# Two cross-attention layers in fp32: the keys' bias sums folded by VectorE and summed by one short product, and the last rows copied in two parts

## The chip, the cores and the metric

The kernel runs on one core of a Trainium2 chip. The metric is the device time of one execution in microseconds (us). Before the change three executions took 582.25, 584.28 and 584.83 us; the median, 584.28, stands for the kernel.

The engines are named as the profile names them: PE (TensorE, matrix products; PEld are its weight loads), DVE (VectorE), ACT (ScalarE), POOL (GpSimd) and SP (SyncE, which here only issues transfers). SBUF is the on-chip memory, 128 partitions wide; PSUM is what PE writes to, in banks of 128 by 512 fp32 numbers.

## The reference

Two layers of cross-attention run one after the other. A batch has 100 tokens of width E = 1024 and 1444 context rows of width L = 512; there are 8 batches. All is fp32.

```
layer 0:  Q = x Wq + bq,  K = ctx Wk + bk,  V = ctx Wv + bv
          x = x + softmax(Q K' / 32, over keys) V Wo + bo
layer 1:  q, k, v in the same way, from the new x, with layer 1's weights
          w = softmax(q k' / 32, over axis 1)          (over the TOKENS, for each key)
          x = layernorm(w v + x) * gamma + beta
```

Layer 1 takes its softmax over the tokens. So what depends on the token alone doesn't cancel in it: the term of the keys' bias, x·(Wq bk) + bq·bk, is needed for each of the 800 tokens. In layer 0 the same term shifts a whole softmax; the kernel still carries it into the shift of the exponent.

## The kernel before, in words

**Products are rearranged.** Scores are (x (Wq Wk') + u) ctx', so the keys are never projected: `weight_products` makes Wq Wk' for each layer ("qk0", "qk1") and Wv Wo for layer 0 ("vo0"), and `queries` multiplies it by x (g0T and g1T in the profile, 512 features by 2 groups of 400 tokens). Large products use seven block products in place of eight (Strassen in Winograd's form): `left_sums`, `right_sums` and `inner_product` have DVE form the sums of blocks, PE the seven products X, Z, Y, W and so on, and DVE and ACT add the results to their places (`add`, `put`).

**Stages in PE's order**, which is the order of the program (`manual_schedule`): qk0, vo0, queries of layer 0, qk1 (137 to 184 us); scores and weighted sums of layer 0 (185 to 319); its output product and the queries of layer 1 (310 to 388, and g_y later); scores and weighted sums of layer 1 with output products between them (388 to 573).

**A batch of attention.** `scores_by_keys` computes the 1444 by 100 scores in 12 blocks of 128 keys (the last has 36), four contraction steps each, into three PSUM banks; blocks stand in two halves of the array at once, so a batch is 184 matmul records (s, L965). It is a generator that stops after each block, except after the very last, after which it goes on to set up the softmax. `weighted_rows` multiplies the weights by the context rows (A, 192 records, L915). `alternated` takes one step of A of batch b and one of s of batch b + 2 in turn.

**The keys' bias.** `key_bias_sums` has DVE (in layer 0 ACT as well, with a transfer that adds the two parts) form kb[p, t] = sum over c of xT[p, c, t] wqbk[p, c], with 128 partitions by 800 tokens. What is wanted is the sum over the 128 partitions, in every partition. `key_bias_rows` (L651 to L657) does that with two products of an all-ones 128 by 128 matrix by 400 columns, and DVE scales each and adds bq·bk while it copies it back to kb (in the profile: PE `kb<-kb,ones` L656, and DVE `kb<-kb,bqbk`; all DVE instructions that go through the object `vector` have line L100, so they are told apart by their tiles).

In layer 0 this happens behind qk1 (L853, L854), ahead of the first scores. In layer 1 it happens inside the scores of batch 0: after 46 of the 48 steps come the two products, then the last two steps (L1472 to L1475), then what remains of the queries (g_y, L1476), then the scores of batch 1.

**Sums in every partition by 32 by 32 blocks.** For other sums the kernel has a second way: `block_sums` (L592) transposes in 32 by 32 blocks and reduces, and `totals` (L603) multiplies the result by `same`, a 0/1 matrix with same[p, j] = 1 where p and j agree modulo 32 (L606). DVE's transpose works on each 32 by 32 block by itself.

**Orders.** PE runs in the program's order. The order of the other engines is a planner's, from its own costs, except where `vector.in_order` is true or `keep_in_program_order` is called: those instructions keep the program's order among themselves. Transfers of the context are all issued on SP's queue in program order (`loaded_in_order`, L862); transfers that add into a tile are POOL's (`transfer_added`, L579). PSUM has two pools: `bank` (6 banks, in which scores and most products live) and `bank2` (2 banks). A bank is taken at the first use of its tile and is free after the last.

**qk1's `between`.** `weight_products` calls `between` (L539, L540) while the inner product W runs, after DVE has formed the operands of the inner product Q (`last`). For qk1 it did nothing. DVE is in the program's order there.

**The end.** `weighted_rows` of the last batch copies its 400 columns (4 chunks of 100 tokens) from PSUM with one ACT copy (L927); `project_last` then multiplies the last 128 rows by wv in three column parts (ol, L1371: 383 + 1, 512 and 129 columns, four contraction steps each, one for a chunk), and DVE, ACT and POOL normalise and store them.

Of the kernel before, what the change touches and what calls it, by code (L numbers as in the profile page):

```python
# [25 lines left out]
F32 = mybir.dt.float32  # L26
AF = mybir.ActivationFunctionType
ALU = mybir.AluOpType
AX = mybir.AxisListType
PE = mybir.EngineType.PE  # L30

P = 128
HP = P // 2
B, T, E = 8, 100, 1024
S, L = 1444, 512
EC, LC = E // P, L // P
NQ = 4
MC = 12
CQ = MC // NQ
GM = 4  # L40
QD = 32
G = 4
GT = G * T
# [5 lines left out]
KEYS = (8, 11, 9, 10, *range(8))  # L49
LAST = (MC - 1) * P  # L50
PAD = S - LAST + QD
SCALE = 1.0 / math.sqrt(E)
# [4 lines left out]
def two_layer_cross_attention(ctx: ExitStack, tc: tile.TileContext, a: dict, out: bass.AP):  # L57
    nc = tc.nc
# [5 lines left out]
    small = ctx.enter_context(tc.tile_pool(name="small", bufs=2))  # L64
# [4 lines left out]
    def bank(name):  # L69
        return psum.tile([P, 512], F32, tag="ps", name=name)  # L70
# [34 lines left out]
    vector = Vector()  # L105


    ones = const.tile([P, P], F32, tag="ones", name="ones")
# [7 lines left out]
    same = const.tile([P, P], F32, tag="same", name="same")  # L116
# [28 lines left out]
    def run(*parts):  # L145

        parts = list(parts)
        while parts:
            parts = [g for g in parts if next(g, parts) is not parts]
# [442 lines left out]
    def block_sums(name, t, sums, late=False):  # L592

        ins = nc.vector.transpose(t, t)
        if late:
            tc.keep_in_program_order(ins)  # L600
        nc.vector.tensor_reduce(sums, t.rearrange("p (c q i) -> p c q i", q=P // QD, i=QD), AX.X, ALU.add)

    def totals(name, sums, n):  # L603

        ps = bank(name)[:, : n * P // QD]
        nc.tensor.matmul(ps, same, sums.rearrange("p c q -> p (c q)"), start=True, stop=True)  # L606
        own = small.tile([P, 2 * EC, P // QD], F32, tag="own", name=f"{name}_own", bufs=1)[:, :n, :]
        mask = quarter.unsqueeze(1).to_broadcast([P, n, P // QD])
        nc.vector.tensor_tensor(own, ps.rearrange("p (c q) -> p c q", q=P // QD), mask, ALU.mult)
        got = const.tile([P, n], F32, tag=name, name=name)  # L610
        nc.vector.tensor_reduce(got, own, AX.X, ALU.add)
        return got

    def quarter_sums(name):
        return small.tile([P, 2 * EC, P // QD], F32, tag="sums", name=f"{name}_sums")

    def bias_products():

        part = small.tile([P, 2], F32, tag="bbs", name="bbs")
        for layer in range(2):  # L620
            prod = small.tile([P, EC], F32, tag="bb", name=f"bb{layer}")
            nc.vector.tensor_tensor(prod, cols[f"L{layer}_xattn_bq"], cols[f"L{layer}_xattn_bk"], ALU.mult)
            nc.vector.tensor_reduce(part[:, layer : layer + 1], prod, AX.X, ALU.add)
        ps = bank("bb_ps")
        nc.tensor.matmul(ps[:, :2], ones, part, start=True, stop=True)
        got = const.tile([P, 2], F32, tag="bqbk", name="bqbk")
        nc.vector.tensor_scalar(got, ps[:, :2], SCALE, None, ALU.mult)
        return got[:, 0:1], got[:, 1:2]

    def key_bias_sums(name, wqbk, tiles=()):  # L630

        acc = to = work.tile([P, B * T], F32, tag="kb", name=name, bufs=1)

        def steps():
            if tiles:
                scaled_sum(tiles, [(xT[:, k, :], wqbk[:, k : k + 1]) for k in range(EC)])
            for k in range(len(tiles), EC):  # L640
                if k == len(tiles):
                    vector.tensor_scalar(to, xT[:, k, :], wqbk[:, k : k + 1], None, ALU.mult)
                else:
                    vector.scalar_tensor_tensor(to, xT[:, k, :], wqbk[:, k : k + 1], to, ALU.mult, ALU.add)
                yield
            if tiles:
                transfer_added(to, tiles[0])

        return acc, steps()

    def key_bias_rows(kb, bqbk):  # L651

        for g in range(B // G):
            rows = kb[:, g * GT : (g + 1) * GT]
            ps = bank(f"kb_{g}")[:, :GT]
            nc.tensor.matmul(ps, ones, rows, start=True, stop=True)  # L656
            vector.tensor_scalar(rows, ps, SCALE, bqbk, ALU.mult, ALU.add)  # L657

    def queries(layer, w, u, between=None):

# [156 lines left out]
    bqbk0, bqbk1 = bias_products()  # L817
# [11 lines left out]
    for g in range(B // G):  # L829
# [9 lines left out]
    gT[0], steps = queries(  # L839
        0, wqk0, totals("u0", sums_u, LC), lambda: block_sums("bvo", acc_o, sums_c[:, EC:, :], late=True)  # L840
    )
    qk1 = weight_products(
        "qk1", "L1_xattn_WqT", "L1_xattn_WkT", E, L, (("L1_xattn_bk", 0), ("L1_xattn_bq", 1)), lambda: None
    )
    run(islice(steps, 2))
    next(qk1)
# [4 lines left out]
    kb0, more = key_bias_sums("kb0", wqbk0[:, :EC], [t[:, : B * T] for t in prob])  # L851
    run(more)
    wqk1, (acc_c, acc_u) = next(qk1)  # L853
    key_bias_rows(kb0, bqbk0)  # L854
    sums = quarter_sums("k1")

    def add_out_bias(e):
# [49 lines left out]
    def weighted_rows(s, layer, c, dst):  # L907

        b, w = s["b"], s["w"]
        ps = bank2(f"A{layer}_{b}")  # L910
        for m in range(MC):
            r = max(keys(m), PAD)
            for k in range(LC):
                for h in both_sides():
                    nc.tensor.matmul(  # L915
                        ps[h * HP : (h + 1) * HP, k * T : (k + 1) * T],
                        c[m // CQ][:r, m % CQ, k * P + h * HP : k * P + (h + 1) * HP],
                        w[:r, m, :],
                        start=(m == 0 and k == 0),
                        stop=(m == MC - 1),  # L920
                        skip_group_check=True,
                    )
                if (m, k) == (MC - 1, LC - 1):
                    src = ps[:, :GT].rearrange("p (c t) -> p c t", t=T)
                    if layer:
                        for to, part in dst:
                            ins = nc.scalar.copy(to, src[:, :, part])  # L927
                            if s["b"] == B - 1:
                                tc.keep_in_program_order(ins)
                    else:  # L930
                        divided(s, ps, dst, src)
                yield
# [13 lines left out]
        nc.vector.reciprocal(r, ps[:, GT : GT + T])  # L946
        nc.vector.tensor_tensor(dst, src, r.unsqueeze(1).to_broadcast([P, LC, T]), ALU.mult)

    def scores_by_keys(s, layer, cT, softmax):

        b = s["b"]
        q = gT[layer][b // G]
        t0 = b % G * T
        banks = [bank(f"s{layer}_{b}_{n}") for n in range(MC // GM)]
        rest = []
        for k in range(LC):
            for m in KEYS:
                whole = keys(m) == P
                n = HP if whole else keys(m)
                for h in both_sides() if whole else one_side():  # L960
                    o = m * P + h * HP if whole else m * P
                    to = banks[m // GM][h * HP : h * HP + n, m % GM * T : (m % GM + 1) * T]
                    if k >= LC - 2 and not whole:
                        rest.append(to)
                    nc.tensor.matmul(  # L965
                        to,
                        cT[k][:, o : o + n],
                        q[:, k, t0 : t0 + T],
                        start=(k == 0 and m % GM == 0),
                        stop=(k == LC - 1 or (k == LC - 2 and not whole)),  # L970
                        skip_group_check=True,
                    )
                if (k, m) != (LC - 1, KEYS[-1]):
                    yield
        w = weight_rows(f"w{layer}_{b}")
        s["w"] = w[:, : MC * T].rearrange("p (c t) -> p c t", t=T)
        nc.gpsimd.memset(s["w"][:PAD, MC - 1, :], 0.0)  # L977
        s["softmax"] = softmax(s, [blocks_of(banks, ms) for ms in ROWS], rest)
        for _ in islice(s["softmax"], LATER.get((layer, b))):
            pass  # L980
        yield
# [408 lines left out]
    batches = [{"b": b} for b in range(B)]  # L1390
# [22 lines left out]
    cT = [list(load_features(0)), list(load_features(1, (2,)))]  # L1413
# [39 lines left out]
    kb1, more = key_bias_sums("kb1", wqbk1)  # L1453
# [4 lines left out]
            next(more, None)  # L1458
    run(more)
    vector.in_order = False  # L1460
    wv1 = weights.tile([P, LC, E], F32, tag="w", name="wv1")
    nc.gpsimd.dma_start(out=wv1, in_=a["L1_xattn_Wv"].rearrange("(c p) e -> p c e", p=P))


    cT = [list(load_features(0, parts=4)), list(load_features(1, (2,), 4))]
    result = out.rearrange("b t e -> (b t) e")
    n = TILES[-1][0] // 6
# [1 line left out]
        loaded_in_order(result[i * n : (i + 1) * n], a["L1_xattn_beta"].partition_broadcast(n))  # L1469
    tiles = [{"t0": t0, "n": n} for t0, n in TILES]  # L1470
    turned = turned_blocks(tiles)
    scores1 = scores_by_keys(batches[0], 1, cT[0], softmax1)  # L1472
    run(islice(scores1, LC * MC - 2))
    key_bias_rows(kb1, bqbk1)
    run(scores1)  # L1475
    run(steps)  # L1476
    run(scores_by_keys(batches[1], 1, cT[1], softmax1))
# [9 lines left out]
    for b in range(B):  # L1487
        parts = []
        for last, _, tokens in SETS:
# [6 lines left out]
            to = homes[last][:, :, lo - tokens.start : hi - tokens.start]  # L1496
# [52 lines left out]
```

## Time and profile before

| | us |
|---|---|
| median of three executions | 584.28 |
| the profiled execution's own time | 581.93 |
| its span, first to last instruction | 580.2 |
| PE busy in the span | 569.4 |
| DVE busy | 429.0 |
| ACT busy | 145.3 |
| POOL busy | 122.6 |
| PE records on the bias products (L656), 8 of them, together | 3.1 |

The profile is one execution. Its times run from the span's start. A row of a timeline has the start, the length, the engine, the line, the operation, the tiles (result <- operands), the shape, and how many instructions were merged; in brackets stands how long the engine had been idle before it and what released it. A matmul's end is modelled and overlaps the next one's start, so distances between starts are what PE's work costs. An fp32 matmul stands as two records. PE's granted clock is 1.00 in every stretch from 185 to 556 us and 0.91 in the last 24 us. Single instructions can be read with a timeline of one engine in a short window; groups of the same instruction with the list of groups.

### The profile page before, as it was taken

The numbers are of one execution on the slowest core, as the hardware profiler recorded it, in microseconds if no ns is written. First come the engines' busy times: TensorE is split into PE (matmuls) and PEld (weight loads), VectorE is DVE, ScalarE is ACT, GpSimd is POOL, SyncE is SP. The second block draws the span as 40 slices with busy tenths as digits, with TensorE's granted clock in tenths as the row PEclk, the third lists the DMA queues.
The fourth block names the chain that finished last, engine by engine and source line by source line (L and its number), as shares of the span: only waits on it lengthen the run. The fifth ranks groups of instructions, "written<-read, shape, count | busy, mean of one in ns | idle before, by whom it ended". The sixth has DMA issues, their size and how long they took to land.

```text
span 580.2 us, 17218 instructions
## 1 busy us (share of the span) xinstructions
PE 569.4 (98%) x7280; PEld 473.4 (82%) x7280; DVE 429.0 (74%) x990; ACT 145.3 (25%) x379; POOL 122.6 (21%) x189
## 2 busy tenths in 40 slices
PE   9999999999999999999999999999999999999994
PEld 8887457678899999999998856677999869959672
DVE  1997579879587684784559786895568769969855
ACT  1331321432250112101211000013333036236532
POOL 3110110221120142052223000000423313404412
PEclk9999999999999999999999999999999999999998
DMA  9959989944399999999999004886899958996704
GB/s 281 313 106 320 311 205 280 311 79 97 68 234 335 348 388 372 331 371 374 366 353 304 2 0 160 263 282 203 247 298 337 361 171 292 295 285 205 204 2 92
DMA packets 74125, 142.83 MB, mean 246 GB/s; under 512 B 8384, under 2 KB 30144, under 8 KB 74048
## 3 DMA queue, kind: packets, MB, share of 16 engines
q1 hardware_dynamic: 66592, 120.62, 60.8%
q0 software_dynamic: 7024, 20.59, 17.9%
q8 instruction: 57, 0.93, 0.6%
q10 hardware_dynamic: 432, 0.52, 0.3%
q14 instruction: 20, 0.16, 0.1%
HBM read 124.28 MB, written 6.03 MB: 225 GB/s over the span
## 4 chain that ended last, share of the span: by engine, by line
PE 76%; issue 6%; DMA 5%; POOL 1%; DVE 1%; ACT 1%; POOLq 0%; DVEq 0%
PE s L965 22%; PE A L915 21%; PE g_x L168 5%; PE qk_x L168 4%; PE o_x L168 3%; PE o_x L1211 3%; DMA vo_L_xattn_bv<-vo_L_xattn_bv 2%; DMA g_t<-xT 2%; PE g_y L168 2%; PE o_y L1211 2%; PE o_y L168 1%; PE qk_z L168 1%; PE qk_y L168 1%; PE o_w L1211 1%; PE o_z L1211 1%
## 5 line engine op out<-in xcount | busy, mean ns | idle before, releaser
L915 PE MATMUL A<-w,c 128*64 128x100 f32 (+1 forms) x3072 | 226.9, 249 | 0.0
L915 PEld LDWEIGHTS A<-w,c 128*64 128x64 f32 (+1 forms) x3072 | 202.4, 137 | 1.7 <-issue 1.7
L965 PE MATMUL s<-g0T,cT 128*64 128x100 f32 (+1 forms) x1472 | 112.8, 250 | 1.1 <-issue 0.8
L965 PE MATMUL s<-g1T,cT 128*64 128x100 f32 (+1 forms) x1472 | 113.5, 250 | 0.3 <-issue 0.3
L965 PEld LDWEIGHTS s<-g0T,cT 128*64 128x64 f32 (+1 forms) x1472 | 100.9, 136 | 2.8 <-issue 2.2
L965 PEld LDWEIGHTS s<-g1T,cT 128*64 128x64 f32 (+1 forms) x1472 | 97.4, 136 | 2.3 <-issue 1.7
L1178 POOL TENSOR_TENSOR part<-w 128x500 f32<-128x500 f32 x16 | 26.9, 1682 | 155.4 <-DVE rtotal L100 88.4
L1158 ACT ACTIVATE w<-w,negmax 128x100 f32<-128x100 f32 x96 | 35.0, 366 | 56.0 <-DVE negmax L100 55.9
L1026 ACT ACTIVATE w<-w 128x400 f32<-128x400 f32 (+2 forms) x32 | 12.0, 442 | 119.6 <-DVE w L100 119.6
L100 DVE STREAM_TRANSPOSE z<-xT 32x256 f32<-32x256 f32 x88 | 38.3, 435 | 1.3
L100 DVE TENSOR_REDUCE most<-s 128x100 f32<-128x400 f32 (+1 forms) x24 | 12.5, 521 | 35.7 <-PE s L965 35.7
L168 PE MATMUL qk_x<-qk 128*128 128x256 f32 x128 | 30.4, 386 | 0.0
L168 PEld LDWEIGHTS qk_x<-qk 128*128 128x128 f32 x128 | 23.9, 195 | 3.1 <-ACT qk L442 0.2
L100 DVE SCALAR_TENSOR_TENSOR w<-s,kb 128x400 f32<-128x400 f32 (+2 forms) x32 | 13.8, 463 | 11.7 <-PE s L965 11.5
L977 POOL MEMSET w<- 68x100 f32 x16 | 3.8, 238 | 68.1 <-PE A L915 28.3
L1158 ACT ACTIVATION_READ_ACCUMULATOR w<-w,negmax 128x1 f32 x96 | 18.0, 188 | 0.0
L676 ACT ACTIVATE g1T<-g_x,k 128x400 f32<-128x400 f32 x4 | 2.4, 593 | 59.4 <-PE g_x L168 59.2
L1181 POOL TENSOR_TENSOR part<-part 128x100 f32<-128x100 f32 x32 | 16.5, 516 | 2.5
L100 DVE TENSOR_TENSOR w<-w,rtotal 128x400 f32<-128x400 f32 (+2 forms) x32 | 15.0, 469 | 1.1
L580 POOL DMA_DIRECT2D qk_L_xattn_bk<-qk_L_xattn_bk x6 | 5.2, 923 | 48.1 <-DMA qk_L_xattn_bk<-qk_L_xattn_bk 20.1
L168 PE MATMUL vo_x<-vo 128*128 128x512 f32 x32 | 15.3, 595 | 0.0
L1330 POOL TENSOR_TENSOR rstd<-rstd,mhalf 128x1 f32<-128x1 f32 (+2 forms) x6 | 8.2, 1370 | 28.2 <-DVE rstd L100 22.3
(448 smaller groups left out, 1031.9 us busy)
## 6 DMA issues: line engine op xcount, KB each, us to landing
c<-in_ctx SPq DMA_DIRECT2D x176, 256.0 KB
cT<-in_ctxT SPq DMA_DIRECT2D x96, 176.0 KB
cT<-in_ctxT SPq DMA_DIRECT2D x32, 370.0 KB
cT<-in_ctxT SPq DMA_DIRECT2D x32, 352.0 KB
cT<-in_ctxT SPq DMA_DIRECT2D x32, 194.0 KB
vo<-in_L_xattn_Wo SPq DMA_DIRECT2D x8, 512.0 KB
qk<-in_L_xattn_WqT SPq DMA_DIRECT2D x8, 512.0 KB
qk<-in_L_xattn_WqT SPq DMA_DIRECT2D x15, 256.0 KB
```

Of the source, the lines that this page charges most:

```text
L100: ins = getattr(nc.vector, op)(*args, **kw)
L168: nc.tensor.matmul(banks[n // per][:, n % per * width : (n % per + 1) * width], lhs[i][:, n * P : (n + 1) * P], rhs[i], start=(fresh and i ...
L580: nc.gpsimd.dma_start(out=to, in_=t, accum_op=ALU.add)
L915: nc.tensor.matmul(ps[h * HP : (h + 1) * HP, k * T : (k + 1) * T], c[m // CQ][:r, m % CQ, k * P + h * HP : k * P + (h + 1) * HP], w[:r, m, :],
L965: nc.tensor.matmul(to, cT[k][:, o : o + n], q[:, k, t0 : t0 + T], start=(k == 0 and m % GM == 0), stop=(k == LC - 1 or (k == LC - 2 and no ...
L977: nc.gpsimd.memset(s["w"][:PAD, MC - 1, :], 0.0)
L1026: nc.scalar.activation(rows, rows, AF.Exp)
L1158: nc.scalar.activation(rows[:, i, :], rows[:, i, :], AF.Exp, bias=negmax[:, i : i + 1], accum_out=total[:, i : i + 1])
L1178: add(part, w[:, 0:5, :], w[:, 5:10, :], ALU.add)
L1181: add(part[:, 0, :], part[:, 0, :], more, ALU.add)
L1211: nc.tensor.matmul(ps[:n, :], lhs[0][:, i, :], rhs[0][:, i, :], start=(fresh and i == 0), stop=(i == 1), skip_group_check=True,)
L1330: nc.gpsimd.tensor_tensor(rstd, rstd, mhalf[:n], ALU.pow)
```

## The change

The two 400-column products with all ones become one product of 25 columns with `same`. For that, DVE first folds kb: it transposes kb in 32 by 32 blocks in place and reduces each block's 32 columns to one, which gives `part`, 128 by 25: partition 32 r + i has, for block n, the sum over quarter r's partitions for token 32 n + i. The product with `same` adds the four quarters. DVE scales the 25 columns and spreads them back: one transpose in 32 by 32 blocks whose input repeats each of the 25 columns 32 times.

The fold is a function of its own, called earlier than the product: in layer 0 in qk1's `between`, in layer 1 after the sums of kb are complete. In layer 1 the product now comes after all 48 score steps of batch 0 (`hold` makes the generator stop after the last block as well). And the last batch's copy of rows is made in two ACT copies of two chunks each.

```diff
-    def key_bias_rows(kb, bqbk):
-
-        for g in range(B // G):
-            rows = kb[:, g * GT : (g + 1) * GT]
-            ps = bank(f"kb_{g}")[:, :GT]
-            nc.tensor.matmul(ps, ones, rows, start=True, stop=True)
-            vector.tensor_scalar(rows, ps, SCALE, bqbk, ALU.mult, ALU.add)
+    def key_bias_parts(kb):
+
+        n = B * T // QD
+        part = small.tile([P, 2 * EC, P // QD], F32, tag="own", name="kb_part", bufs=1)
+        part = part.rearrange("p c q -> p (c q)")[:, :n]
+        vector.transpose(kb, kb)
+        vector.tensor_reduce(part, kb.rearrange("p (n i) -> p n i", i=QD), AX.X, ALU.add)
+        return part
+
+    def key_bias_rows(kb, part, bqbk):
+
+        n = B * T // QD
+        ps = bank("kb")[:, :n]
+        nc.tensor.matmul(ps, same, part, start=True, stop=True)
+        vector.tensor_scalar(part, ps, SCALE, bqbk, ALU.mult, ALU.add)
+        spread = part.unsqueeze(2).to_broadcast([P, n, QD])
+        vector.transpose(kb.rearrange("p (n i) -> p n i", i=QD), spread)
...
+    kb0_part = []
     qk1 = weight_products(
-        "qk1", "L1_xattn_WqT", "L1_xattn_WkT", E, L, (("L1_xattn_bk", 0), ("L1_xattn_bq", 1)), lambda: None
+        "qk1", "L1_xattn_WqT", "L1_xattn_WkT", E, L, (("L1_xattn_bk", 0), ("L1_xattn_bq", 1)),
+        lambda: kb0_part.append(key_bias_parts(kb0)),
     )
...
-    key_bias_rows(kb0, bqbk0)
+    key_bias_rows(kb0, kb0_part[0], bqbk0)
...
                         for to, part in dst:
-                            ins = nc.scalar.copy(to, src[:, :, part])
-                            if s["b"] == B - 1:
-                                tc.keep_in_program_order(ins)
+                            for ks in (range(2), range(2, LC)) if s["b"] == B - 1 else (range(LC),):
+                                k0, k1 = ks[0], ks[-1] + 1
+                                ins = nc.scalar.copy(to[:, k0:k1, :], src[:, k0:k1, part])
+                                if s["b"] == B - 1:
+                                    tc.keep_in_program_order(ins)
...
-    def scores_by_keys(s, layer, cT, softmax):
+    def scores_by_keys(s, layer, cT, softmax, hold=False):
...
-                if (k, m) != (LC - 1, KEYS[-1]):
+                if hold or (k, m) != (LC - 1, KEYS[-1]):
                     yield
...
+    part = key_bias_parts(kb1)
...
-    scores1 = scores_by_keys(batches[0], 1, cT[0], softmax1)
-    run(islice(scores1, LC * MC - 2))
-    key_bias_rows(kb1, bqbk1)
+    scores1 = scores_by_keys(batches[0], 1, cT[0], softmax1, hold=True)
+    run(islice(scores1, LC * MC))
+    key_bias_rows(kb1, part, bqbk1)
     run(scores1)
```

## The prediction

> **What bounds the kernel now.** I read the page's engine table first, then the list of who waited for whom, then the timeline of each engine around the instructions that the change touches.
>
> ```profile
> PE 569.4 (98%) x7280; PEld 473.4 (82%) x7280; DVE 429.0 (74%) x990; ACT 145.3 (25%) x379; POOL 122.6 (21%) x189
> ```
>
> TensorE (PE) is busy in 569.4 of 580.2 us and sits on the end chain nearly throughout. In the list of waits PE has four entries, 3.1 us together, none of them in front of the bias products. So a microsecond of PE work taken out is a microsecond of span, as long as what PE needs next is there earlier too. Around the bias products PE's timeline in layer 0 is
>
> ```profile
> 184.01 1.51 PE L656 MATMUL kb<-kb,ones 128*128 128x400 f32 x4
> 185.44 1.77 PE L965 MATMUL s<-g0T,cT 128*64 128x100 f32 x36
> ```
>
> and in layer 1
>
> ```profile
> 388.06 7.78 PE L965 MATMUL s<-g1T,cT 128*64 128x100 f32 x176
> 395.77 1.61 PE L656 MATMUL kb<-kb,ones 128*128 128x400 f32 x4
> 397.31 0.56 PE L965 MATMUL s<-g1T,cT 128*64 128x100 f32 x8
> 397.80 1.61 PE L168 MATMUL g_y<-xT,qk 128*128 128x400 f32 x4
> ...
> 403.37 8.12 PE L965 MATMUL s<-g1T,cT 128*64 128x100 f32 x184
> 411.32 0.34 PE L915 MATMUL A<-w,c 128*64 128x100 f32 x4
> ```
>
> Columns: start, length, engine, line, operation, count. One fp32 product stands as two records. What counts is from start to start, since a record's end overlaps the next: the two bias products hold PE from 184.01 to 185.44 = 1.43 us in layer 0. In layer 1 they cut one batch's scores in two: from 388.06 to g_y at 397.80 = 9.74 us, where an uncut batch takes 411.32 - 403.37 = 7.95.
>
> **Step 1: the short product.** The nearest rows are the existing products with the same 0/1 matrix (L606), with 48 and with 16 moving columns:
>
> ```profile
> 318.42 0.32 PE L606 MATMUL k<-k_sums,same 128*128 128x48 f32 x2
> 318.67 0.31 PE L915 MATMUL A<-w,c 128*64 128x100 f32 x2
> ```
>
> ```profile
> 99.66 0.29 PE L606 MATMUL u<-u_sums,same 128*128 128x16 f32 x2
> 99.80 0.92 PE L168 MATMUL g_x<-xT,qk 128*128 128x400 f32 x2
> ```
>
> Start to start: 0.25 us before a half-array product, 0.14 before a full-array one. The Trainium skill (TensorE: Matmul & The Clock Gate, Back-to-back issue gap) lets a product of 1 to 64 columns cost about 60 cycles, 25 ns, so 0.05 us for two records; the rows say three to five times that, and I take the rows. By the page the whole sum would be some 0.3 us better.
>
> Layer 0: scores follow, as A follows in the 48-column row, so 1.43 - 0.25 = 1.18 us gained (1.43 - 0.14 = 1.29 at best).
>
> Layer 1: an uncut batch 7.95, plus 0.09 for the switch to a full-array product (last score to kb is 0.18 us where score pairs are 0.086 apart), plus 0.14 to 0.25 for the product: 8.18 to 8.29, against 9.74. I take 1.50 us. Moving the last two score groups ahead of the product (`hold`) is in this number: the cut's second switch goes.
>
> **Step 2: the fold on DVE**, a transpose and a reduction of 128x800, once per layer. The rows of 1024 columns:
>
> ```profile
> 91.01 1.23 DVE L598 STREAM_TRANSPOSE qk_L_xattn_bk<-qk_L_xattn_bk 128x1024 f32<-128x1024 f32 x1
> 92.28 1.22 DVE L601 TENSOR_REDUCE c_sums<-qk_L_xattn_bk 128x32 f32<-128x1024 f32 x1
> 93.41 0.41 DVE L100 TENSOR_TENSOR vo<-vo,vo_w_y 128x256 f32<-128x256 f32 x1
> ```
>
> With the rows of 512 columns (702 and 686 ns) the slope is 1.04 ns a column, so 800 take 1.00 and 0.99 us long, and start to start 1.27 - 0.23 = 1.04 and 1.13 - 0.23 = 0.90: 1.94 us. In layer 0 this is pinned into DVE's order where qk1 calls `between`, after the operands of the inner product Q are made and before this:
>
> ```profile
> 174.68 0.41 DVE L100 TENSOR_TENSOR qk<-qk,qk_w_y 128x256 f32<-128x256 f32 x1
> 176.23 0.75 DVE L100 TENSOR_TENSOR qk<-qk,qk_w_x 128x256 f32<-128x256 f32 x2 [1.13 <-PE qk_w_x L168]
> 177.98 0.42 DVE L100 TENSOR_TENSOR qk<-qk,qk_q_x 128x256 f32<-128x256 f32 x1 [1.01 <-PE qk_q_x L168]
> ```
>
> Queued behind the fold are the adds of qk_w_y and qk_w_x, then qk_q_x. DVE waits 1.13 + 1.01 = 2.14 us for PE there; the fold ends near 176.6, the three adds near 177.65, and qk_q_x can't start before 177.98 anyway. Cover 2.14, cost 1.94: nothing on PE. Two more waits of 0.26 and 0.47 us stand before the last adds at 182.76. The fold's own input landed about 156 (POOL issues the transfer at 150.78, 5.2 us to landing). A rule speaks against this step: the skill (VectorE: DVE Perf Modes, Rules for kernel authors) calls `tensor_reduce` the slowest DVE operation, not for a hot path. Were the fold on the path twice, 3.9 us would turn the gain into a loss of 1; the waits say it isn't. In layer 1 it comes after the adds ending at 390.75, is done by 392.7, and its product runs near 396.1: 3.4 us to spare.
>
> **Step 3: scaling and spread on DVE.** Two scalings of 128x400 go; one of 128x25 (about 0.16 us, as the one-column TENSOR_SCALAR rows of 155 ns) and one transpose of 128x800 with a repeated input come, about 1.0 us. The repeated input is the unknown: 1.0 at the rate of the other transposes; at worst I allow 4.0; it can't be under 0.7, the 512-column row. I take 1.0: the nearest rows for a repeated input are the products w<-w,rtotal, which read one value 100 times and take 575 ns for 400 columns, and those with two full inputs (xT<-xT,o_x) take 566.
>
> ```profile
> 186.14 1.17 DVE L100 TENSOR_SCALAR kb<-kb,bqbk 128x400 f32<-128x400 f32 x2
> 192.71 0.47 DVE L100 TENSOR_REDUCE most<-s 128x100 f32<-128x300 f32 x1 [5.40 <-PE s L965]
> ```
>
> ```profile
> 396.75 1.30 DVE L100 TENSOR_SCALAR kb<-kb,bqbk 128x400 f32<-128x400 f32 x2 [5.99 <-PE kb L656]
> ```
>
> In layer 0 DVE idles 5.40 us after it and kb is first read at 198.97. In layer 1 the softmax of batch 0 is queued behind it: scaling starts near 396.5, spread ends near 397.7, against 398.0 before, so the softmax is a little earlier while PE is 1.5 us earlier. The weights of batch 0 are ready at 405.7; PE wants them at 411.32 - 1.50 = 409.8: 4.1 us of cover, enough even for a 4 us spread. Cost: nothing.
>
> **Step 4: the last copy in two.**
>
> ```profile
> 565.14 0.49 ACT L927 COPY A1T<-A 128x400 f32<-128x400 f32 x1 [2.66 <-PE A L915]
> ...
> 565.68 1.56 PE L1371 MATMUL ol<-wv_first,A1T 128*128 128x384 f32 x4 [0.59 <-ACT A1T L927]
> ```
>
> PE starts when the 400 columns are copied. Copies of 176 and 224 columns take 313 and 345 ns, so 200 take 0.33: PE starts 0.16 us earlier. An existing pair (224 then 176) lasts 0.55 us together, so the second half is there near 565.7, and PE asks for it at 566.8. Behind it on ACT is the scaling of tile 4's rows (565.53), 0.1 us later; its store waits on POOL's power until 568.5. If PE waited for both parts, this would be +0.07. I take 0.16: the last stage then ends on PE (DVE waits 1.78 us for it at 572.0).
>
> **Sum.** 1.18 + 1.50 + 0.16 = 2.84 us. The profiled execution took 581.93 (span 580.2), so it would take 579.1. The median shown is 584.28, of 582.25, 584.28 and 584.83: 584.28 - 2.84 = 581.4. Since that median lies above the mean of the four executions (583.3), I put the forecast at 581.2.
>
> **Rivals.**
> *Part of layer 0's gain is lost again* (0.20): two places are tight. The score banks: at 184.01 four of six are still held by qk1's X pair and Q's x and y. The short product and the first score bank take the two free ones; the next two are wanted at about 184.85 and 185.55, and DVE's adds free them at 184.6 and 185.2: 0.2 to 0.3 us. A fold over 3.0 us (1.94 + the spare 0.35 + 0.26 + 0.47) would push that. And the features of batch 2 land about 2.7 us before use (my count of the load queue's bytes against its order), 1.5 after the change. For it: the DMA engines are never free there (share 1.0, 325 to 380 GB/s). Against it: both still hold on paper. If all of 1.18 goes: 584.28 - 1.66 = 582.6.
> *Slower* (0.13): PE's own code. 57 transfers of 16 KB feed instructions, and PE stands still for 0.2 to 0.8 us some 1.4 us after several of them, with no releaser (191.1, 196.9, 224.5, 230.2, 236.5, 258.6, 449.0), about 2.5 us in all. The skill (Runtime: NRT & Kernel Launch, Instruction fetch mechanics) says that crossing a block is mostly hidden; this trace says mostly, not always. Removing instructions shifts every later block against the loads. If all of the some 30 blocks of the loaded stages stalled 0.35 us, 10.5 in place of 2.5: 581.4 + 8 = 589. It decides from 5.8 us more of stalls. For it: nobody places these blocks. Against it: the average should stay.
> *The copy or the reordering does nothing*: 0.16 or 0.1 less, inside the noise.
>
> **Chances.** Full gain 0.67, own range 579.3 to 582.9; partly lost 0.20; slower 0.13. What a measurement of this kernel can tell from no change is about 0.5%, 2.9 us: the sum lies on that line. Faster by more 0.52, within 0.35, slower 0.13. The range 579.3 to 584.2 leaves out the slow rival and a little on either side.
>
> **What would show it.** Right: about 0.25 us from the kb product to the scores in layer 0; g_y some 8.25 us after the first score of batch 0 in layer 1; no PE wait on DVE at 184 to 187; the fold filling DVE's two waits at 175 to 178; ol starting 0.43 us after A's last record ends, not 0.59. Wrong: a PE wait in front of the second or third score bank or of batch 2's scores, a spread of several us, or PE standing still without a releaser for over 4 us in all.

## The result and the profile after

The changed kernel takes 579.77 us (median of 13 runs, 578.58 to 581.22). The kernel before, run beside it 13 times, takes 582.72 us (580.61 to 584.83). The ratio is 0.9942 with a 95% interval of 0.9928 to 0.9957, which is 2.5 to 4.2 us less. The forecast was 581.2 us in a range of 579.3 to 584.2, with a full gain of 2.84 us. The profiled execution took 579.72 us with a span of 577.9 us, 2.2 us less than the one before (581.93 and 580.2).

The page's engine table after the change:

```profile
PE 566.7 (98%) x7276; PEld 472.5 (82%) x7276; DVE 432.7 (75%) x994; ACT 145.4 (25%) x380; POOL 122.6 (21%) x189
```

PE lost 2.7 us of busy time, and DVE gained 3.7 us. The four large products of two records each have become two short ones. PE's timeline at the bias product of layer 0:

```profile
183.63 0.30 PE L664 MATMUL kb<-kb_part,same 128*128 128x25 f32 x2
183.86 3.31 PE L979 MATMUL s<-g0T,cT 128*64 128x100 f32 x72
```

From start to start it is 0.23 us where it was 1.43 us, and nothing waits on either line: no idle time stands in brackets. PE's timeline in layer 1:

```profile
387.48 8.12 PE L979 MATMUL s<-g1T,cT 128*64 128x100 f32 x184
395.53 0.40 PE L664 MATMUL kb<-kb_part,same 128*128 128x25 f32 x2
395.77 5.62 PE L168 MATMUL g_y<-xT,qk 128*128 128x400 f32 x16
...
409.27 0.34 PE L927 MATMUL A<-w,c 128*64 128x100 f32 x4
```

Batch 0's scores are one stretch of 184 records now. From the first score to g_y it is 395.77 - 387.48 = 8.29 us where it was 9.74 us. DVE's timeline, first at the fold in layer 0:

```profile
174.31 1.01 DVE L100 STREAM_TRANSPOSE kb<-kb 128x800 f32<-128x800 f32 x1
175.35 0.99 DVE L100 TENSOR_REDUCE kb_part<-kb 128x25 f32<-128x800 f32 x1
...
177.61 0.42 DVE L100 TENSOR_TENSOR qk<-qk,qk_q_x 128x256 f32<-128x256 f32 x1 [0.29 <-PE qk_q_x L168]
```

The fold takes 1.94 us (174.31 to 176.25, where the adds begin). DVE's two waits for PE of 1.13 and 1.01 us have shrunk to one of 0.29 us. It is still DVE that waits for PE there, so the fold is covered. Then DVE at the scaling and the spread in layer 1:

```profile
395.97 0.25 DVE L100 TENSOR_SCALAR kb_part<-kb,bqbk 128x25 f32<-128x25 f32 x1 [3.85 <-PE kb L664]
396.25 1.01 DVE L100 STREAM_TRANSPOSE kb<-kb_part 128x800 f32<-128x800 f32 x1
...
402.08 0.57 DVE L100 TENSOR_TENSOR w<-w,rtotal 128x400 f32<-128x400 f32 x1
```

The spread, whose input is one value repeated 32 times, takes 1.01 us. The last line is the first group of weights that A needs: it is ready at 402.65, 6.6 us before PE's first A record at 409.27. The end of the kernel on PE:

```profile
563.47 2.20 PE L1385 MATMUL ol<-wv_first,A1T 128*128 128x384 f32 x6 [0.42 <-ACT A1T L941]
```

The wait for the copy is 0.42 us where it was 0.59 us. The list of waits of PE (engine, what was waited for, us in total, times, longest) has a new line, though:

```profile
PE A L927 <- issue: 1.1, 2, 0.6
...
PE s L979 <- DMA cT<-in_ctxT: 0.8, 1, 0.8
```

The scores of batch 2 wait for that batch's features near 200 us. PE's timeline there, first before and then after the change:

```profile
189.79 13.44 PE L965 MATMUL s<-g0T,cT 128*64 128x100 f32 x291
```

```profile
195.76 4.12 PE L979 MATMUL s<-g0T,cT 128*64 128x100 f32 x92
200.70 2.16 PE L979 MATMUL s<-g0T,cT 128*64 128x100 f32 x45 [0.82 <-DMA cT<-in_ctxT]
```

The wait is 0.8 us in these views, whose record ends are modelled; it is 1.0 us from start to start. So the terms are there in full, 1.20 + 1.45 + 0.17 = 2.82 us, and in this one execution a wait takes most of layer 0's term back.

A ledger of PE's start times, after less before, shows where the 2.2 us come from. PE is 0.37 us early when it comes to layer 0's product: a wait of 0.4 us for g_t near 116 us, which the change doesn't touch, is missing. Layer 0's product adds -1.21. In the rest of layer 0, +1.00 comes back: the wait for batch 2's features is +1.03, and pauses of PE that come and go nearly cancel. Layer 1's product adds -1.45, the pauses behind it -0.02, the last copy -0.17.

By pauses I mean places in the scores and A products at which PE stands still and nothing releases it. Starts of neighbouring half-array records lie 0.043 us apart there, and a step of over 0.19 us is counted, whole. There were 3.3 us of them before, and 2.9 us after, beside the wait for the features.

### The profile page after: what moved, and what is told of

The parts are those of the page before. It is cut to its first block, busy times and chain, and to the rows that moved or that the text cites. A ratio compares the mean times of both kernels' runs of the same rounds, so it can differ in the third digit from the quotient of the medians.

```text
span 577.9 us, 17212 instructions
## 1 busy us (share of the span) xinstructions
PE 566.7 (98%) x7276; PEld 472.5 (82%) x7276; DVE 432.7 (75%) x994; ACT 145.4 (25%) x380; POOL 122.6 (21%) x189
## 4 chain that ended last, share of the span: by engine, by line
PE 90%; DMA 4%; issue 2%; DVE 1%; POOL 1%; ACT 1%; SPq 1%; DVEq 0%; POOLq 0%
PE A L927 22%; PE s L979 19%; PE qk_x L168 7%; PE g_x L168 6%; PE vo_x L168 4%; PE o_x L168 3%; PE o_x L1225 3%; PE g_y L168 3%; DMA cT<-in_ctxT 3%; PE qk_y L168 2%; PE qk_z L168 2%; PE o_y L1225 2%; DMA c<-in_ctx 2%; PE o_y L168 1%; PE qk_w L168 1%
## 5 line engine op out<-in xcount | busy, mean ns | idle before, releaser
L927 PEld LDWEIGHTS A<-w,c 128*64 128x64 f32 (+1 forms) x3072 | 199.0, 137 | 3.1 <-issue 2.8
L979 PEld LDWEIGHTS s<-g0T,cT 128*64 128x64 f32 (+1 forms) x1472 | 97.4, 136 | 2.5 <-issue 1.3
```

The source lines that it names most:

```text
L927: nc.tensor.matmul(ps[h * HP : (h + 1) * HP, k * T : (k + 1) * T], c[m // CQ][:r, m % CQ, k * P + h * HP : k * P + (h + 1) * HP], w[:r, m, :],
L979: nc.tensor.matmul(to, cT[k][:, o : o + n], q[:, k, t0 : t0 + T], start=(k == 0 and m % GM == 0), stop=(k == LC - 1 or (k == LC - 2 and no ...
```

## The experiments

The first theory says that the three terms on PE come off the time one for one, and that what DVE and ACT took over is hidden. The second says that the features of batch 2, which used to land just in time, take most of layer 0's term back. Beside these stood the question whether PE's pauses, the slow rival of the prediction, decide the time. "The changed kernel" is the kernel after the change; a group is a set of kernels run side by side. Each kernel's ratio is to the kernel before, run on the same chip; its median is 582.93, 584.02 and 583.09 us for the first, second and third group.

**One layer alone** (first group). Both kernels leave the last copy in one piece; each keeps the old bias products in the other layer.

```diff
 layer0_only
-    part = key_bias_parts(kb1)
...
-    run(islice(scores1, LC * MC))
-    key_bias_rows(kb1, part, bqbk1)
+    run(islice(scores1, LC * MC - 2))
+    key_bias_rows_old(kb1, bqbk1)
 layer1_only
-        lambda: kb0_part.append(key_bias_parts(kb0)),
+        lambda: None,
...
-    key_bias_rows(kb0, kb0_part[0], bqbk0)
+    key_bias_rows_old(kb0, bqbk0)
```

> The change in layer 0 alone: fold in qk1's between, one 25-column product, spread; layer 1's bias product and the last copy stay as before. Theory 1 (PE's sum): what PE no longer does comes off one for one, 1.2 us less than before (ratio 0.998). Theory 2 (the load of batch 2's features): the profile after shows PE waiting 0.82 us for those features, so layer 0 gives back most of its gain there: 0.3 to 0.5 us less than before (ratio 0.9993), and the profile again has a wait of PE for cT near 200 us. Under both, PE goes from the product to the scores within 0.25 us.

> The change in layer 1 alone: fold after kb's sums, product after all scores of batch 0, spread; layer 0 and the last copy as before. Both theories: 1.5 us less than before (ratio 0.9974), from the first score of batch 0 to g_y 8.3 us in place of 9.7, no new wait of PE. A rival in which layer 1's gain is lost to later stages would give under 0.7.

Layer 0 alone: 581.7 us (22 runs), 0.9972 (0.9959 to 0.9985), so -1.6 us (-0.9 to -2.4). Layer 1 alone: 581.83 us (14 runs), 0.9984 (0.9967 to 1.0), so -0.9 us (0 to -1.9). The terms of the sum, -1.20 and -1.45, lie in these intervals. In the traces the two stretches are those of the changed kernel where a layer is changed (0.23 and 8.29 us) and those of before where it isn't (1.44 and 9.74 us). The two gains and the copy's 0.17 make 2.7 us, about what the whole change brings. Layer 0 alone brought its whole term. But that is no test of the second theory, since this kernel's profile hardly has the wait. PE's list for layer 0 alone:

```profile
PE s L985 <- issue: 2.1, 3, 1.0
PE A L935 <- issue: 1.6, 3, 1.0
```

No line for cT stands in it; at batch 2's first score PE stood still for 0.2 us and not for 1.0.

**The features earlier** (first group). Two blocks of batch 2's features are issued ahead of the last quarter of batch 0's rows.

```diff
-    c0, more = list(load_rows(0)), load_features(2)
+    rows, more = load_rows(0), load_features(2)
+    c0 = [next(rows) for _ in range(NQ - 1)]
     cT.append([next(more)])
...
+    cT[2].append(next(more))
+    c0 += rows
     cT[2] += more
```

> The changed kernel, with two feature blocks of batch 2 issued ahead of the last quarter of batch 0's context rows (the same transfers in another order). Theory 2: the wait of PE for cT near 200 us goes and up to 0.8 us comes off the changed kernel (ratio to before 0.9930 to 0.9937 where the changed kernel has 0.9942). Theory 1: no wait that matters was there, so the time of the changed kernel stays (0.9942).

579.72 us (22 runs), 0.9953 (0.9938 to 0.9967): no faster than the changed kernel (0.9942), as the first theory expected. The wait for the features is gone from the list of waits of PE, but the lines without a releaser have grown:

```profile
PE A L927 <- issue: 3.2, 4, 1.8
PE s L979 <- issue: 1.2, 2, 0.9
```

By the count above the pauses are 6.2 us in this execution, against 2.9 in the changed kernel. The cure worked on the wait and brought no time; what took its place isn't shown.

**Without layer 0's bias sums** (first group, again in the second). In layer 0 the bias of a key's row is the same for all keys of a softmax and cancels, so its sums, their loads and their product are left out.

```diff
-    kb0, more = key_bias_sums("kb0", wqbk0[:, :EC], [t[:, : B * T] for t in prob])
-    run(more)
...
-    key_bias_rows(kb0, kb0_part[0], bqbk0)
...
-        bias, shift = kb0[:, b * T : (b + 1) * T], shift[:, :T]
-        vector.scalar_tensor_tensor(shift, shift, SCALE, bias, ALU.mult, ALU.add)
-        vector.tensor_tensor(shift, bias, shift, ALU.subtract)
+        shift = shift[:, :T]
+        vector.tensor_scalar(shift, shift, -SCALE, None, ALU.mult)
```

> The changed kernel without any bias sums for the keys in layer 0 (kb0): no sums over xT, no fold, product or spread; the exponent's shift is minus the scaled maximum, which is what the formula comes to, since the bias cancels in a softmax over the keys. It takes 0.23 us off PE against the changed kernel and some 9 us off DVE, ACT and POOL. Theory 1: 0.2 us less than the changed kernel (ratio 0.9938 to before). Theory 2: nothing off, or a longer wait for cT (0.9942). If DVE's or POOL's work in layer 0 had a hidden price, clearly more than 0.3 us.

> The changed kernel without layer 0's bias sums, once more. If PE's sum is all (0.23 us), the ratio to before is 0.9938 beside 0.9942, inside the noise, and the 1.6 us by which it was ahead of the changed kernel before was chance in PE's pauses. If less work on DVE, ACT and POOL is worth something by itself, it is again ahead by 1 us or more (0.992 or lower).

578.14 us (6 runs), 0.9926 (0.9899 to 0.9953), and 578.1 us (6 runs), 0.9907 (0.9885 to 0.9928). Beside the changed kernel's 0.9942 above and 0.9933 in the second group this is 0.9 and 1.5 us less, where PE loses one product of 0.23 us. The intervals overlap each time, but both point the same way. The queue of loads shows one more difference. First this kernel's, then the changed kernel's timeline of SP from 176 to 195 us:

```profile
178.17 9.93 SPq L872 DMA_DIRECT2D c<-in_ctx  x13
188.50 5.59 SPq L872 DMA_DIRECT2D cT<-in_ctxT  x8
```

```profile
178.47 14.97 SPq L875 DMA_DIRECT2D c<-in_ctx  x13
193.55 1.43 SPq L875 DMA_DIRECT2D cT<-in_ctxT  x3
```

The loads of rows are through 5 us earlier, and batch 2's features (cT) are issued at 188.5 and not at 193.55. PE doesn't wait for them in either profile of this kernel, where it waited for 1.0 us in the changed one. So 0.23 + 1.0 us is of the size of the 0.9 and 1.5 us; the pauses beside it were 1.2 and 3.5 us. That the missing wait is the cause isn't shown: in the kernel with the features earlier its removal alone brought nothing, and here DVE, ACT and POOL have less to do as well.

**The changed kernel again** (second group).

> The changed kernel itself once more, as the mark for the run without kb0 on the same chip, and for a second sample of PE's pauses without a releaser. Ratio to before 0.994, profiled pauses anywhere from 1 to 6 us.

580.06 us (6 runs), 0.9933 (0.9911 to 0.9955). The wait for the features is there again, 0.94 us: both profiled executions of this kernel have it.

**The fold's reduction five times** (second group, run once, so only the traces are compared). Layer 0's reduction is repeated; the result is the same.

```diff
-        vector.tensor_reduce(part, kb.rearrange("p (n i) -> p n i", i=QD), AX.X, ALU.add)
+        for _ in range(1 + again):
+            vector.tensor_reduce(part, kb.rearrange("p (n i) -> p n i", i=QD), AX.X, ALU.add)
```

> The changed kernel with the fold's reduction in layer 0 done five times over (same result), so 3.6 us more on DVE in qk1. By the prediction's account of the cover (0.35 us left before qk_q_x, some 1 us more before PE wants the next operand of Q at 180.4) PE now waits some 2.2 us for DVE between 180 and 185. If the cover is larger than I read it, PE waits less than 1 us; if there is none, 3.6.

PE's timeline at the place:

```profile
182.23 1.16 PE L168 MATMUL qk_q_x<-qk 128*128 128x128 f32 x8 [2.31 <-DVE qk L100]
183.23 1.86 PE L168 MATMUL qk_q_w<-qk 128*128 128x128 f32 x8
184.88 1.91 PE L168 MATMUL qk_q_y<-qk 128*128 128x128 f32 x8
```

The 4.1 us more of DVE work make PE wait for 2.31 us. The cover is there, and it has an end. But the second and third product behind the wait take 1.86 and 1.91 us, where the first takes 1.16. The table of stretches (busy PE, PEld, DVE, ACT, POOL, then the granted clock, the DMA share, GB/s) says why:

```profile
182.23:183.36 1.13, 1.13 (x9) 1.13 (x10) 1.13 (x5) 0.00 (x0) 0.00 (x0) 1.00 1.14 276
183.36:186.77 3.41, 3.41 (x18) 3.41 (x17) 2.87 (x8) 0.00 (x0) 0.33 (x1) 0.50 1.02 312
186.77:188.00 1.23, 1.23 (x15) 1.20 (x15) 1.23 (x3) 0.00 (x0) 0.72 (x2) 1.00 0.99 285
```

The granted clock is 1.00 during the wait and for 1.1 us after it, then 0.50 for 3.41 us, then 1.00 again. PE's start times put the loss at 2.47 us for the wait and 1.77 us for the slow clock, 4.2 together; half of 3.41 is 1.7. At the end only 1.7 us of it are left in the span (579.6): batch 2's features are no longer waited for (1.0), and the pauses are 2.0 us where they were 2.9.

**The spread seven times** (second group, run once), in layer 1 alone.

```diff
-        vector.transpose(kb.rearrange("p (n i) -> p n i", i=QD), spread)
+        for _ in range(1 + again):
+            vector.transpose(kb.rearrange("p (n i) -> p n i", i=QD), spread)
```

> The changed kernel with layer 1's spread done seven times over (same result), 6.2 us more on DVE ahead of batch 0's softmax. By the account of the cover (weights ready 4.2 us ahead of their first use) PE waits some 2 us for DVE ahead of the first A of layer 1; with no cover 6.

Six more spreads, 6.2 us of DVE work, cost PE nothing that the trace can show, where a wait of some 2 us was expected. DVE's timeline, and below it PE's at the first A record:

```profile
397.14 5.20 DVE L100 STREAM_TRANSPOSE kb<-kb_part 128x800 f32<-128x800 f32 x5
...
409.56 0.57 DVE L100 TENSOR_TENSOR w<-w,rtotal 128x400 f32<-128x400 f32 x1
```

```profile
410.24 0.39 PE L928 MATMUL A<-w,c 128*64 128x100 f32 x4
```

The first weights are ready at 410.13, and PE takes them at 410.24 with no wait. It is 0.97 us later than in the changed kernel, but the scaling ahead of the spread (396.86, against 395.97) was 0.89 us later already. The cover is some 6.6 us, not the 4.1 us of the prediction, and these six spreads just fill it.

**A quarter less traffic** (third group). In the attention every second batch takes the rows of the batch before it, so those rows aren't loaded and the output isn't the reference's; PE's work is the same. Once on the kernel before and once on the changed one:

```diff
-        c, *cT = got or loaded(load_rows(b), *([load_features(b + 2, parts=4 if layer else 2)] if nxt else []))
+        features = [load_features(b + 2, parts=4 if layer else 2)] if nxt else []
+        if b % 2:
+            c, cT = held[0], loaded(*features)
+        else:
+            c, *cT = got or loaded(load_rows(b), *features)
+        held[:] = [c]
```

> The kernel before with fewer transfers: in both layers odd batches reuse the context rows of the batch before them in the weighted sums, so a quarter of the attention's load traffic is left out, and the weighted sums of odd batches are not the reference's. PE's work and order are the same. If PE's pauses without a releaser (2.6 us in layer 0 in the profiled execution of before) come from crowded transfers, they fall under 0.5 us and the time to 2 to 4 us under before; if they belong to PE's program itself, they stay at 2 to 3 us.

> The changed kernel with the same fewer transfers. With pauses and load waits out of the way the change should show its bare PE sum: 2.8 us less than the quiet kernel before (1.2 in layer 0, 1.45 in layer 1, 0.17 at the end), with a narrow spread. If the change were worth more than the sum by itself, over 3.3 us.

The two are 580.55 us (13 runs), 0.9956 (0.9939 to 0.9973), and 576.03 us (6 runs), 0.9899 (0.9873 to 0.9926). Their quotient is 0.9943, the ratio of the two kernels with all of the traffic, but it may lie between 0.991 and 0.997 (an estimate from the two intervals), and the medians are 4.5 us apart. So it agrees with the sum of 2.8 us and is no sharp test of it. The table of stretches, first of the kernel before and then of the quiet kernel before:

```profile
205.00:250.00 45.00, 44.34 (x1024) 43.77 (x1022) 31.53 (x89) 7.97 (x16) 13.94 (x22) 1.00 1.02 366
```

```profile
205.00:250.00 45.00, 43.52 (x1006) 43.13 (x1004) 29.73 (x84) 7.97 (x16) 12.58 (x18) 1.00 0.66 228
```

The DMA share is 0.66 where it was 1.02. The two signs that were named beforehand disagree. The pauses of the quiet kernel before are 4.3 us in its profiled execution, against 3.3, which speaks against crowded transfers as their cause. But its runs are 2.6 us (1.6 to 3.6) faster than before, and by the ratios the quiet changed kernel is 2.0 to 2.5 us faster than the changed one, with pauses of 0.5 us beside a wait for the features of 0.9 us. So less traffic saves time, and one profiled execution can't say where. Whether full DMA engines make PE pause stays open.

**Both together** (third group): no bias sums in layer 0, and the features earlier; the two edits shown above.

> The changed kernel without layer 0's bias sums and with the two feature blocks of batch 2 issued earlier. If what the run without kb0 gained (1.6 to 2 us over the changed kernel) is the load queue's head start, moving loads forward once more adds little: 578 us, ratio 0.991 to 0.993. If the wait for batch 2's features were still there in part, up to 0.5 us better.

576.43 us (6 runs, 575.6 to 577.21), 0.9894 (0.9872 to 0.9915). It is faster than the 578 us that were expected, and its pauses are 1.0 us. Its interval lies below that of the kernel with the features earlier alone (0.9938 to 0.9967). Beside the kernel without the sums (0.9926 and 0.9907) the intervals overlap, so what the order of loads adds here isn't shown.

## Why the prediction was right, step by step

*PE's work comes off one for one.* It held. The sum was 1.18 + 1.50 + 0.16 = 2.84 us. The trace shows 1.20 + 1.45 + 0.17 = 2.82, the medians 2.95, the ratio 3.4 (2.5 to 4.2). The layers alone and the quiet pair agree with it within wider intervals.

*The forecast itself* was 1.4 us too high, nearly all of it from its starting point. It was made from 584.28, the median of three runs, taken down by 0.2 on account of the other executions. The 13 runs of before have their median at 582.72, and 582.72 - 2.84 is 579.9, against 579.77. That the base's error still left the result 0.5 us inside the lower end of the range (579.3) is luck.

*Step 1.* The rows of this kernel were the right source: 0.23 us before half-array products and 0.24 before full-array ones (395.53 to 395.77). The 0.05 us for two records that the prediction worked out from the skill's page would have been wrong by 0.2 us on each. In layer 1 the longer end of 8.18 to 8.29 came true, because I had allowed 0.14 us before a full-array product.

*Step 2.* It held to the hundredth, 1.94 us, with 0.29 us of DVE's waits left over. The fold repeated shows that the cover has an end: at 6.0 us of fold PE lost 2.3 to 2.5 us, so it was 3.6 us or a little more where I had counted 3.0. It also shows that the loss is dearer than the wait, since a slow clock follows it. The rule against `tensor_reduce` doesn't bear on this: it took 0.99 us for 800 columns, no longer than the transpose, and was hidden.

*Step 3.* The spread took 1.01 us, as assumed. The scaling took 0.25 us and not 0.16, hidden. The cover was measured to the wrong row: I took the last weights of batch 0 (405.7), but PE's first A records read only the first group, which comes 2.5 us sooner. I erred to the safe side.

*Step 4.* 0.17 us against 0.16; the pair of copies lasts 0.55 us, as foreseen.

*The rival of a lost part.* The score banks kept pace: PE shows no idle time from 183.63 to 187. The features didn't, and a PE wait in front of batch 2's scores was one of my signs of being wrong. I had them land 2.7 us ahead of use, 1.5 after the change, from a count of bytes in the load queue. The trace also records the updates of the semaphore by which a transfer tells that it has landed. They give, for the first feature block of batch 2:

| profile | landed, us | PE could use it, us | ahead of use, us |
|---|---|---|---|
| before | 201.53 | 201.60 | 0.1 |
| layer 1 alone | 199.65 | 201.29 | 1.6 |
| layer 0 alone | 198.67 | 198.62 | -0.1 |
| changed | 200.56 | 199.67 | -0.9 |
| changed, again | 200.19 | 199.38 | -0.8 |
| spread seven times | 200.40 | 199.18 | -1.2 |

So my count was 2.4 to 2.6 us too kind for the changed kernel and for before. And the landing shifts by 1.9 us between executions whose layer 0 is the same (before and layer 1 alone; changed and layer 0 alone). In before and in the changed kernel, 1.5 us lie between the end of the block's last packet and the last update of its semaphore; the rest is an error of the count. The wait is real, and still the medians show the whole sum: had 1.0 us come off it, 1.8 us would be left, which lies outside the interval of 2.5 to 4.2. What makes up for it isn't settled. Removing the wait by an earlier issue brought nothing, while the kernels without layer 0's sums, which don't have it either, were 0.9 and 1.5 us faster, of which the product itself is 0.23.

*The slow rival.* It needed 5.8 us more of pauses. The two profiles of the changed kernel have 2.9 and 4.5 us where before has 3.3. The largest count is 6.2 us, in the kernel with the earlier features. My mark for "wrong", over 4 us in all, was too tight: four profiles of kernels with the change or part of it passed it, and the medians of the three of them that were run repeatedly stayed in line with the sum. Over thirteen profiled executions I found 75 pauses, the waits for features among them. 71 of them end 1.21 to 1.61 us after one of the 16 KB transfers of the instruction queue has ended. These transfers come some 5.5 us apart in layer 0, and only 7% of all starts in the scores and A products lie in that stretch behind one. The other four stand at batch 2's first score, where the features had just landed. So PE is most likely waiting for its own code, which is inferred from these distances and not from a wait that the trace names. What decides which block comes late stays open: a quarter less traffic made the runs faster without taking the pauses out of both profiles, and no run moved the code alone.

## What to carry to other kernels

On an engine that is busy 98% of the span, a change is costed from start to start in the timeline of that engine alone, and what moves to other engines is checked against their waits; here that gave 2.84 us against 2.82. A gain of half a per cent needs a base of more than three runs, since the base was the largest error of the forecast. When the bound engine gets earlier, look for the load that was just in time, and take its landing from the semaphore's updates, in more than one execution, not from its last packet. Pauses counted in a single profiled execution say little about a kernel: two of the same kernel had 2.9 and 4.5 us.

## What the runs showed of the hardware

A wait of PE of 2.31 us, with PE busy before and behind it, was followed 1.1 us later by 3.41 us at a granted clock of 0.50, which cost 1.77 us more. A wait of 1.4 us from start to start, in the profile of the spread seven times, was followed by no such drop. The Trainium skill (TensorE: Matmul & The Clock Gate, Part 1: The HAM clock gate) lets the clock fall after an idle window of about 3.4 us; here two thirds of that was enough, so the measurement decides.

A 32 by 32 transpose with a repeated input is no dearer than one with a full input: 1.01 us against 1.00 for 128x800.

A feature block was usable 1.5 us after its last packet had ended, in the profiles of before and of the changed kernel. The Trainium skill (DMA: Bandwidth & Descriptors, Anatomy of one DMA — SWDGE (gpsimd) path) gives a transfer that GpSimd issues a fixed cost of about 2.0 us, most of it after the last byte; these blocks are issued on SyncE's queue, so for them the measured 1.5 us stands.
